# A four-layer graph kernel on one core: GpSimd clears an unused tile behind each indirect gather

## The chip, the cores and the metric

The kernel runs on one core of one Trainium2 chip. The metric is the device time of one execution in microseconds (us). The time shown for a kernel is the median of its timed runs; a separate execution is recorded by the hardware profiler, and all rows of the profile come from that one.

## The reference, cut to what matters

There are 16 graphs (b = 0 to 15) of 1024 nodes with 64 channels, and each has a sparse 1024x1024 adjacency. Four layers follow each other, each of the form x = layernorm(x + f(x, adj)).

```python
x = layernorm(x + (adj @ (x @ W) + bias))                       # layer 0
x = layernorm(x + L1(x, adj, nodemask))                         # layer 1, below
x = layernorm(x + proj(three times: h = relu(adj @ (h @ Wl + bl))))   # layer 2
x = layernorm(x + (adj @ x > 0.5))                              # layer 3
```

Layer 1 is the one that matters here. For each node it drops some neighbours by their rank (the "dilation"), sorts the remaining neighbours' values channel by channel, takes a weighted sum of three quantiles (0.25, 0.5, 0.75; a quantile between two sorted values is interpolated), adds the node itself, and applies a two-matrix perceptron with ReLU.

## The kernel before, in words

**Tiles.** The nodes of a graph are ranked by their number of neighbours and cut into eight tiles of 128 nodes. Tile t has room for KS[t] neighbours (31 down to 11). The tiles are worked in five groups per graph, `GROUPS = ((0,), (6, 7), (2, 3), (4, 5), (1,))`, so there are 80 groups in all.

**Steps of a graph.** `words_of` loads the adjacency, transposes it on TensorE, packs neighbours into words and does layer 0 (SP loads L417; TensorE L439, L464, L536; ScalarE L441, L539; VectorE L526). `front` makes the list of neighbours of each node (`idx`, `packed`) and writes the layer's input, with two extra columns that name the dropped neighbours, as a table to DRAM (L584). Then for each group:

- `gathered` (L808): GpSimd issues one indirect DMA per neighbour slot (L815). Each fetches 128 table rows of 66 floats, one for every node of the tile, into the group's buffer g. Slots that only few nodes use are fetched together into small `stage` tiles by the same helper; SP copies them to their places (L841) after VectorE has filled those places with a large number (L835).
- `masked` (L847): VectorE finds the dropped neighbours in the gathered rows (L862, L864), and ScalarE adds a large number to them (L868).
- `quantiles` (L891): VectorE runs a sorting network over the slots (L906), with s as its second buffer.
- `summed` (L916): ScalarE weighs the sorted slots (L932), TensorE adds them (L936), and the sum leaves PSUM (L949, L951).

`back` does the rest of layer 1 and layers 2 and 3 (TensorE L1207, L1141, L377; VectorE L1147).

**What sets the order.** Each step is a Python generator that yields the cost it expects; a heap with hand-set due times (`start`, `LENGTHS`, `add`) merges all generators into one program, so each engine has a fixed order of instructions, made before the run. A group's gathers are due two groups ahead of its sort. There are four g buffers for the 80 groups: the gathers of a group go into the buffer of the group four earlier and wait until its L936 (and L906) are done with it. GpSimd has nothing else to do in this stretch: its order is 2064 gathers in a row, 129 per graph (1952 into g, 112 into stage). Waits of a gather, where it has any: on the buffer, on the table, on the index list, and on the completion of the gather eight earlier, since the gathers use eight semaphores in turn.

Of the kernel before, what the change touches and what calls it, by code (L numbers as in the profile page):

```python
# [10 lines left out]
F32 = mybir.dt.float32  # L11
# [4 lines left out]
U8 = mybir.dt.uint8  # L16
# [4 lines left out]
P = 128  # L21
# [132 lines left out]
def kernel(  # L154
# [18 lines left out]
    nc = tc.nc  # L173
    B, N, C = x.shape
    H = w1.shape[1]
    NL = wl.shape[0]
    T = N // P
# [9 lines left out]
    const = ctx.enter_context(tc.tile_pool(name="const", bufs=1))  # L187
# [4 lines left out]
    act = ctx.enter_context(tc.tile_pool(name="act", bufs=1))  # L192
# [64 lines left out]
    top = const.tile([P, T, K], F32, name="top")  # L257
    nc.vector.memset(top, 0.0)
    flags = const.tile([1, B + 1], I32, name="flags")
    qw = const.tile([P, Q], F32, name="qw")  # L260
    ntau = const.tile([P, Q], F32, name="ntau")
    for s, (tau, w) in enumerate(zip(TAUS, QWEIGHTS)):
# [65 lines left out]

    mask_u8 = const.tile([B * T, P], U8, name="mask_u8")
    nc.scalar.dma_start(mask_u8, nodemask.rearrange("b (t p) -> (b t) p", p=P))  # L330
    mask_f = const.tile([B * T, P], F32, name="mask_f")
    nc.vector.tensor_copy(mask_f, mask_u8)
    mask = const.tile([P, B * T], F32, name="mask")
    pm = ps.tile([P, HALF], F32, tag="mm", name="pm", bufs=2)
# [447 lines left out]
    def group(g):  # L782

        n = max(KS[t] for t in GROUPS[g])
        lo, hi = RANKS[n]
        return GROUPS[g], n, lo, hi + 1 - lo

    def slots(g, buf, a, e):

        tiles, n, _, _ = group(g)  # L790
        return buf[:, :len(tiles) * n * R].rearrange("p (k t c) -> p t k c", k=n, c=R)[:, :, a:e, :]

    def packs_of(g):

        return [q for q, pack in enumerate(PACKS)
                if pack and g == min(h for h, tiles in enumerate(GROUPS) for p in pack if p[0] in tiles)]

    def shares_of(g):

        found = {}  # L800
        for q, pack in enumerate(PACKS):
            for t, k, m, first in pack:
                if t in GROUPS[g]:
                    found.setdefault((t, m, first, q // 2), []).append((q, k))
        return [(t, m, first, v[0][0], [k for _, k in v])
                for (t, m, first, _), v in sorted(found.items())]

    def gathered(st, g):  # L808
        tiles, n, _, _ = group(g)
        while "table" not in st:  # L810
            yield 0.5
        nt = len(tiles)
        st["g", g] = buf = srt.tile([P, KMAX * R], F32, tag="x", name="g", bufs=4)
        def gather(dst, index):
            nc.gpsimd.indirect_dma_start(  # L815
                out=dst, out_offset=None, in_=st["table"],
                in_offset=bass.IndirectOffsetOnAxis(ap=index, axis=0))

        whole = [(i, t, k) for i, t in enumerate(tiles) for k in range(n)
                 if k < len(ROWS[t]) and ROWS[t][k] == P]  # L820
        for j, (i, t, k) in enumerate(whole):
            if j == FIRST:
                for q in packs_of(g):
                    if q % 2 == 0:
                        st["stage", q // 2] = small.tile([P, 2 if PACKS[q + 1] else 1, R], F32,
                                                         tag=f"stage{q // 2}", name="stage", bufs=1)
                    gather(st["stage", q // 2][:, q % 2], st["packed"][:, q:q + 1])
                    yield 1.0
            gather(buf[:, (k * nt + i) * R:(k * nt + i + 1) * R], st["idx"][:, t, k:k + 1])
            yield 1.0  # L830
            if j == FIRST + LAG:
                for i2, t2 in enumerate(tiles):
                    full = ROWS[t2].count(P)
                    if full < n:
                        nc.vector.memset(slots(g, buf, full, n)[:, i2], BIG)  # L835
                for t2, m, first, q, ks in shares_of(g):

                    dst = buf[:m, :n * nt * R].rearrange("p (k t c) -> p k t c", t=nt, c=R)
                    dst = dst[:, ks[0]:ks[-1] + 1:max(ks[-1] - ks[0], 1), tiles.index(t2)]
                    src = st["stage", q // 2][first:first + m, q % 2:q % 2 + len(ks)]  # L840
                    nc.sync.dma_start(dst, src)  # L841

            st["in", g] = sum(j >= max(FIRST + LAG, max(x for x, w in enumerate(whole) if w[0] == i2))
                              for i2 in range(nt))
        st["all in", g] = True
# [403 lines left out]
    for b in range(B):  # L1249
        ready = start(b * G - 2) - BEFORE  # L1250
        add(ready - LISTS - WORDS, words_of(state[b]), WORDS / WORDS_STEPS)
        add(ready - LISTS - (LEAD if b else EARLY), front(state[b]), LISTS / LISTS_STEPS)
        add(start((b + 1) * G) + AFTER, back(state[b]), BACK / BACK_STEPS)
        for g in range(G):
            q = b * G + g
            st = state[b]
            count = sum(KS[t] for t in GROUPS[g])
            many = sum(ROWS[t].count(P) for t in GROUPS[g]) + len(packs_of(g))
            add(start(q - 2), gathered(st, g), (start(q - 1) - start(q - 2)) / (many + 1))
            half = (start(q) - start(q - 1)) * (PAIRS if len(GROUPS[g]) > 1 else MASKS)  # L1260
            add(start(q) - half, masked(st, g), 0.9 * half / (1.5 + 0.4 * count + 2.1 * len(GROUPS[g])))
            n = max(KS[t] for t in GROUPS[g])
            cost = 0.2 + sum((len(GROUPS[g]) * x[4] * x[8] * C + 151) / 960 for x in network(n))
            add(start(q), quantiles(st, g), (start(q + 1) - start(q)) / (cost + 0.1))
            add(start(q + 1) + SUMS, summed(st, g))
# [50 lines left out]
```

## Time and profile before

| What | Value |
|---|---|
| Timed runs | 3179.41 us median of 3 (3177.02 to 3182.76) |
| Span of the profiled execution | 4328.2 us |
| Mean granted TensorE clock in it | 0.764 |
| TensorE matmul busy | 2647.8 us, 61% |
| VectorE busy | 2822.0 us, 65% |
| ScalarE busy | 1914.0 us, 44% |
| GpSimd busy | 2160.8 us, 50% |

The profiled execution's own time is known only as its span, from its first to its last instruction; no time of it from outside is given. That span is 4328.2 - 3179.41 = 1148.8 us longer than the median of the timed runs, so shares of the span cannot be taken over to the timed runs as they are; durations of single instructions and the spacing of instructions on one engine are what is read from it. In rows of groups, "<-" in front of tiles means "written from", the number after x is the count, then come busy us, mean ns of one, and the idle time of the engine before them with what ended it. In timeline rows the columns are start us, us, engine, line, operation, tiles, count, and in brackets the idle time before. "issue" is idle time in which nothing that the profile shows was waited for; "remote" and "another core or an unknown queue" are waits whose releaser the profile could not name.

### The profile page before, as it was taken

To read this page: it belongs to the slowest core of one execution; us is meant where nothing else is said; L and a number is where in the kernel's file an instruction comes from. 1 tells how busy PE (TensorE), PEld (TensorE's weight loads), DVE (VectorE), ACT (ScalarE), POOL (GpSimd) and SP (SyncE) were. 2 spreads that over 40 slices of the span, in tenths; PEclk is the share of its full clock that TensorE was granted. 3 is DMA by queue.
4 is the path that set the end of the run, shared out by engine and by line. 5 is a ranking of instruction groups with operands and counts; after the bars stand their busy time and mean duration, and the time that the engine had idled before them with its cause. 6 is when DMAs were issued, how large, how long until landed. Compare 5 with 4: busy or idle time off the path is not lost.

```text
span 4328.2 us, 46055 instructions
## 1 busy us (share of the span) xinstructions
PE 2647.8 (61%) x13765; PEld 1635.7 (38%) x13766; DVE 2822.0 (65%) x6935; ACT 1914.0 (44%) x6153; POOL 2160.8 (50%) x2078
## 2 busy tenths in 40 slices
PE   6034285675848567584755758476575848456478
PEld 5023152443525244352533435253343525233243
DVE  6058383865849486594857668485766859476671
ACT  2034352634536264453535455363545536253641
POOL 1715626455454645546465464546545554645600
PEclk8566597787969778796877879687787969768688
DMA  3212121322222132222213222231322222111210
GB/s 107 42 50 70 34 67 37 104 54 78 73 71 84 40 101 56 78 77 74 77 39 90 64 83 76 65 84 40 100 60 79 78 80 71 39 57 24 62 43 3
DMA packets 169056, 282.54 MB, mean 65 GB/s; under 512 B 99485, under 2 KB 102112, under 8 KB 166880
## 3 DMA queue, kind: packets, MB, share of 16 engines
q1 hardware_dynamic: 67584, 142.01, 9.9%
q0 software_dynamic: 66048, 69.88, 9.1%
q10 hardware_dynamic: 35168, 67.62, 4.1%
q8 instruction: 114, 1.87, 0.2%
q14 instruction: 142, 1.16, 0.1%
HBM read 204.33 MB, written 71.44 MB: 64 GB/s over the span
## 4 chain that ended last, share of the span: by engine, by line
another core or an unknown queue 28%; DVE 25%; PE 23%; ACT 16%; issue 7%; DMA 0%; ACTq 0%; DVEq 0%
DVE g L906 7%; PE mm L1207 7%; DVE s L906 7%; ACT g L868 6%; ACT ones_at L974 3%; PE ax L464 3%; ACT ones_at L975 2%; PE tp L439 2%; PE mm L377 2%; PE pa L936 2%; PE mm L1196 2%; ACT g L932 1%; PE mm L1141 1%; DVE top L707 1%
## 5 line engine op out<-in xcount | busy, mean ns | idle before, releaser
L815 POOL DMA_INDIRECT g<-table,idx x1952 | 2045.4, 1048 | 1919.7 <-PE pa L936 666.8
L1207 PE MATMUL mm<-adjB,msg 128*128 128x512 f32 x1536 | 769.6, 621 | 109.1 <-issue 82.4
L936 PE MATMUL pa<-g,ident 128*128 128x128 f32 (+1 forms) x1600 | 376.0, 360 | 430.1 <-ACT g L932 300.5
L868 ACT ACTIVATE g<-g,bias 128x64 f32<-128x64 f32 (+9 forms) x2272 | 596.8, 341 | 47.9 <-DVE bias L864 29.2
L906 DVE TENSOR_TENSOR s<-g 128x256 f32<-128x256 f32 (+9 forms) x944 | 531.3, 588 | 64.5 <-ACT g L868 55.5
L936 PEld LDWEIGHTS pa<-g,ident 128*128 128x128 f32 x1600 | 312.3, 248 | 574.0 <-ACT g L932 347.1
L906 DVE TENSOR_TENSOR g<-s 128x256 f32<-128x256 f32 (+8 forms) x864 | 473.4, 573 | 9.0 <-DVE s L906 3.0
L932 ACT ACTIVATE g<-g,w 128x64 f32<-128x64 f32 x1552 | 397.8, 341 | 17.2 <-DVE w L912 13.6
L1207 PEld LDWEIGHTS mm<-adjB,msg 128*128 128x128 f32 x1536 | 268.7, 197 | 301.1 <-issue 270.7
L1147 DVE TENSOR_TENSOR u<-mm,mb 128x512 f32<-128x512 f32 x32 | 22.1, 691 | 463.1 <-remote 313.5
L464 PE MATMUL ax<-at,xt 128*64 128x128 f32 x1920 | 284.5, 310 | 17.4 <-issue 17.4
L377 PE MATMUL mm<-adjB,x 128*64 128x512 f32 x512 | 272.6, 666 | 36.3 <-issue 31.3
L979 PE MATMUL mm<-ones_at,pieces 128*64 128x512 bf16 x768 | 213.0, 420 | 119.0 <-ACT ones_at L975 77.1
L464 PEld LDWEIGHTS ax<-at,xt 128*64 128x64 f32 x1920 | 250.2, 158 | 81.2 <-issue 79.1
L439 PE MATMUL tp<-ident,arow 128*128 128x128 f32 x1024 | 181.7, 309 | 156.2 <-remote 66.4
L399 DVE TENSOR_REDUCE ln_v<-sq 128x8 f32<-128x512 f32 x64 | 43.6, 681 | 296.4 <-issue 156.8
L439 PEld LDWEIGHTS tp<-ident,arow 128*128 128x128 f32 x1024 | 140.9, 162 | 205.1 <-issue 131.7
L441 ACT COPY at<-tp 128x512 f32<-128x512 f32 x240 | 139.0, 580 | 177.2 <-remote 122.3
L906 DVE TENSOR_TENSOR g<-g,s 128x256 f32<-128x256 f32 (+5 forms) x432 | 199.1, 464 | 15.1 <-remote 5.0
L906 DVE TENSOR_TENSOR g<-g 128x256 f32<-128x256 f32 (+8 forms) x304 | 200.7, 660 | 11.2 <-remote 4.0
L1219 PE MATMUL mm<-ident,tT 64*128 64x64 f32 x128 | 25.7, 295 | 293.9 <-ACT tT L380 207.4
L1210 ACT ACTIVATE hlT<-mm 128x512 f32<-128x512 f32 x96 | 57.4, 598 | 296.4 <-PE mm L1207 123.7
(225 smaller groups left out, 4361.9 us busy)
## 6 DMA issues: line engine op xcount, KB each, us to landing
arow<-in_adj_dram SPq DMA_DIRECT2D x128, 512.0 KB
adjd<-at ACTq DMA_DIRECT2D x120, 512.0 KB
adjB<-adjd SPq DMA_DIRECT2D x15, 4096.0 KB
g<-table,idx POOLq DMA_INDIRECT x1952
table<-xc ACTq DMA_DIRECT2D x16, 264.0 KB
xt<-in_x_dram SPq DMA_DIRECT2D x16, 256.0 KB
out_dram<-y SPq DMA_DIRECT2D x16, 256.0 KB
stage<-table,packed POOLq DMA_INDIRECT x112
```

What stands on the lines that cost most here:

```text
L377: nc.tensor.matmul(pa[:C, :], src[:, m, :], adjT[:, h * TH:(h + 1) * TH, m, :], start=(m == 0), stop=(m == T - 1))
L439: nc.tensor.transpose(pt[:, i * P:(i + 1) * P], a[:, j * P:(j + 1) * P], ident)
L441: nc.scalar.copy(at[:, h * TH:(h + 1) * TH, :], pt.rearrange("p (i n) -> p i n", n=P))
L464: nc.tensor.matmul(self.bank[:C, cols], self.xt[:, m + 1, :], at[:, m, :], start=(m == 0), stop=(m == T - 1))
L815: nc.gpsimd.indirect_dma_start(out=dst, out_offset=None, in_=st["table"], in_offset=bass.IndirectOffsetOnAxis(ap=index, axis=0))
L868: nc.scalar.activation(v, v, AF.Identity, bias=bias[:m, i, k:k + 1])
L906: nc.vector.tensor_tensor(box(bufs[mode >> 1 & 1], d, run, sd, count), box(bufs[mode >> 3], a, run, sa, count), box(bufs[mode >> 2 & 1], b ...
L932: nc.scalar.activation(slots(g, bufs[0], lo + r, lo + r + 1)[:, i, 0, :C], slots(g, bufs[at[r]], lo + r, lo + r + 1)[:, i, 0, :C], AF.Iden ...
L936: nc.tensor.matmul(pa[:, :(e - k) * nt * C], ident, rows_.rearrange("p (k c) -> p k c", c=R)[:, :, :C], start=(j == 0), stop=(j == len(run ...
L974: nc.scalar.activation(ones_at, iota, AF.Abs, bias=st["minus"][:, s:s + 1])
L979: nc.tensor.matmul(bank[:C, :], pieces[:, i, s, :], ones_at[:, h * HALF:(h + 1) * HALF], start=(s == 0 and i == 0), stop=False)
L1207: nc.tensor.matmul(pg, msg[:, m, :], adjT[:, h * TH:(h + 1) * TH, m, :], start=(m == 0), stop=(m == T - 1))
```

## The change

The helper `gather`, which issues all indirect gathers, also issues a GpSimd memset of a tile named `pause`: 128 partitions of 256 bytes, type uint8, which nothing reads. There are as many memsets as gathers, 2064. To make room, a tile of constants that is used once at the start, `mask_f` (512 bytes per partition), moves from the pool of constants to a slot that is shared with the tiles tagged "u" of `back`.

```diff
@@ -257,6 +257,7 @@
     flags = const.tile([1, B + 1], I32, name="flags")
+    pause = const.tile([P, 2 * P], U8, name="pause")
     qw = const.tile([P, Q], F32, name="qw")
@@ -328,7 +329,7 @@
-    mask_f = const.tile([B * T, P], F32, name="mask_f")
+    mask_f = act.tile([B * T, P], F32, tag="u", name="mask_f")
     nc.vector.tensor_copy(mask_f, mask_u8)
@@ -815,6 +816,7 @@
             nc.gpsimd.indirect_dma_start(
                 out=dst, out_offset=None, in_=st["table"],
                 in_offset=bass.IndirectOffsetOnAxis(ap=index, axis=0))
+            nc.gpsimd.memset(pause, 0)
```

In the built program every gather is followed by one memset on GpSimd. Each memset but the first waits for GpSimd's own semaphore, since it overwrites what the memset before it wrote. The order of instructions on TensorE, VectorE, ScalarE and SP is the same as before.

## The prediction

> **What bounds the kernel now.** I read the page first, for busy shares and the chain of waits that ended last, then the groups of GpSimd, then its timeline, then a table of stretches.
>
> ```profile
> span 4328.2 us, 46055 instructions
> another core or an unknown queue 28%; DVE 25%; PE 23%; ACT 16%; issue 7%; DMA 0%; ACTq 0%; DVEq 0%
> ```
>
> On this page no engine bounds anything: the busiest is at 65%, and the longest part of the chain is waits without a named releaser. GpSimd, the only engine that the change touches, is not in the chain. But the profiled span is 1148.8 us longer than the timed median of 3179.41, and 28% of it, 1212 us, are those nameless waits. One of them in ScalarE's timeline:
>
> ```profile
> 107.53 0.33 ACTq L532 DMA_DIRECT2D adjd<-at  x1
> 165.70 0.21 ACT L539 CAST hi<-tp 128x64 f16<-128x64 f32 x1 [57.65 <-remote]
> ```
>
> L539 waits for matmuls (L536) that the records end at 108.2, and goes on at 165.7. GpSimd issues gathers all the while (110 in a row from 96.0 to 234.0). Such waits lie nearly all in runs of gathers. In the timed run they must be nearly absent, since 4328 - 1212 = 3116 is already below its 3179. So the engines' own pace, not the chain, says what bounds the timed run:
>
> ```profile
> L815 POOL DMA_INDIRECT g<-table,idx x1952 | 2045.4, 1048 | 1919.7 <-PE pa L936 666.8 <-issue 566.6 <-DVE s L906 272.9
> L815 POOL DMA_INDIRECT stage<-table,packed x112 | 113.0, 1009 | 35.0 <-issue 34.7 <-ACT at L441 0.3
> ```
>
> There are 2064 gathers, 2158 us of busy time and 601 us of "issue", about 0.3 us ahead of nearly every gather. The rest of the idle time, 1353 us, waits mostly for a free buffer (L936, L906). The stretches (busy us of PE, PEld, DVE, ACT, POOL with counts, then granted clock, DMA share, GB/s):
>
> ```profile
> 2156.40:2193.50 37.10, 34.67 (x184) 21.50 (x182) 35.81 (x74) 21.23 (x80) 29.43 (x26) 1.00 0.27 68
> 2197.00:2221.00 24.00, 5.42 (x23) 4.69 (x23) 0.00 (x0) 3.56 (x15) 18.19 (x20) 0.57 0.19 32
> 96.00:4116.00 4020.00, 2417.51 (x12660) 1498.03 (x12658) 2672.62 (x6485) 1821.06 (x5889) 2158.24 (x2064) 0.76 0.24 67
> 4116.00:4328.20 212.20, 171.41 (x557) 87.00 (x557) 83.54 (x208) 69.70 (x205) 0.12 (x1) 0.85 0.06 23
> ```
>
> Beside a busy VectorE (35.81 of 37.10 us) a gather is issued every 37.10/26 = 1.43 us; beside an idle one every 1.25 us (2217.54, 2218.79, 2220.03 in the timeline). The gathers begin at 96.0 and the last ends 212 us before the end. The timed run has the same edges if I take them over: 3179.4 - 96.0 - 212.1 = 2871 us are left for 2064 gathers, **1.39 us each**. That is less than the 1.43 of a dense stretch, and only 111 us more than what the profile's mean pace needs (2158 + 601 = 2760 us). So in the timed run GpSimd has nearly no slack. VectorE has little more: 2673 busy us of the 2871, 93%. Both are bounds; TensorE (2418) and ScalarE (1821) are behind.
>
> **The change, part by part.** (1) It removes nothing. (2) It adds 2064 memsets of 128x256 bytes to GpSimd, one between any two gathers. (3) It moves no instruction of another engine, since their order is fixed and is the same in both programs. (4) mask_f moves to a slot of the tag "u": VectorE's copy (L332) runs once at the start, and the slot's next user (L1147) first runs at 560 us. I cost this at nothing: the slot is empty in the first 500 us, which is its cover; without it, one copy would wait once.
>
> What one memset costs has no row. The nearest ones are GpSimd's first instructions:
>
> ```profile
> 0.34 0.10 POOL L1302 MEMSET const-float32-0.0<- 128x1 f32 x1
> 0.37 0.10 POOL L1302 MEMSET const-float32-1.0<- 128x1 f32 x1
> ...
> 1.08 0.97 POOL L212 IOTA iota<- 128x1024 f16 x1
> 2.03 0.28 POOL masks.py:199 TENSOR_SCALAR_AFFINE_SELECT ident<-ident 128x128 f32<-128x128 f32 x1
> 2.27 0.20 POOL L215 MEMSET tri<- 128x128 f16 x1
> 2.43 0.18 POOL L231 IOTA wordkey<- 128x64 int32 x1
> ```
>
> From one start to the next: 0.03 us for 1 element, 2.43 - 2.27 = 0.16 for 128, 0.95 for 1024. That is about 0.9 to 1.0 ns per element, and the 128x128 memsets last 0.205 us in f32 and 0.195 in f16, so elements count, not bytes. 256 elements then take 0.03 + 255 x 0.9 to 1.0 ns = 0.26 to 0.29 us; were it bytes, 256 of them are the 0.16 us of the f16 tile. I take 0.26. Bounds: nothing, if the memset falls into the 0.30 us of "issue" that is there anyway; and 0.26 + 0.30 = 0.56 us, if the memset gets such a gap of its own. The value nearest to the rows stands between; the ends are kept as rivals. Its wait is for the memset before, over a microsecond old, so it holds nothing up. Queued behind each memset is the next gather; who waits for that is the masking (L862, then L868), the SP copies from stage (L841), and so the sort (L906).
>
> The Trainium skill (Perfetto Trace Analysis, GPSIMD Engine Instruction) says that recorded spans of GpSimd are not to be trusted and that spacing of starts should be used; the tri memset shows it, 0.20 us long and 0.16 us to the next start. By durations the memset would be 0.10 + 255 x 0.75 ns = 0.29 us, and the sum 62 us higher. The skill (SBUF — State Buffer, Who interferes with whom) also says that a VectorE instruction with two SBUF inputs, which L906 is, holds up a GpSimd instruction that reads SBUF but not one that only writes; no row shows a memset beside a busy VectorE. If the rule failed and each memset were stretched as gathers are (1.43 - 1.25 = 0.18 us), it would cost 372 us more.
>
> **The sum.** 2064 x 0.26 = 537 us on GpSimd. What hides them: if gathers keep the profile's mean pace, 111 us of waits for buffers in the timed run, so 3179 + 537 - 111 = 3605. If GpSimd is already full, nothing but a small return: VectorE's 2673 us then lie in about 3340 us, 80% instead of 93%, and gathers get faster by 0.18/0.97 x 0.13 = 0.024 us, so 3179 + 2064 x (0.26 - 0.024) = 3666. I take the middle, **3635 us**. By the bytes' price of 0.16 it would be 3400 to 3460, by 0.29 3670 to 3730. GpSimd becomes the only bound; VectorE then idles at the masking step, waiting for gathers. In the profiled execution the same 537 us meet 1353 us of buffer waits, so its span may grow far less, and the sum is not to be read from it.
>
> **Rivals.**
>
> - *The memset hides in the gap.* If the 0.30 us ahead of a gather are the queue's work on it and run beside the memset, the pace grows by 0 to 0.1 us: 3179 to 3385. For it: the gap is constant (0.30 in nearly all rows). Against it: memsets and iotas at the start follow each other with no gap, so GpSimd's queue runs ahead of them and is not what they wait for.
> - *The change doesn't do what it says.* If timed gathers are faster than recorded ones, GpSimd has slack, VectorE is the bound, and the pauses only shorten buffer waits. It needs a pace below 1.39 - 0.26 = 1.13 us; the shortest in the trace is 1.25. Result: 3179.
> - *A gap of its own.* 0.56 us each: 3179 + 2064 x 0.56 - 111 = 4224; in part, 3850 and up.
> - *Faster.* The nameless waits lie in runs of gathers. If the timed run has some, spacing the gathers shortens them. Place: ScalarE's and VectorE's waits for TensorE. Price: VectorE's idle time between the first and last gather, 2871 - 2673 = 198 us at most; half of it gives 3080. It decides only if pace and pause together fit into 3080 - 308 = 2772 us, 1.34 us per gather, which needs a timed gather pace of 1.08 us with my memset, or 1.25 with a memset of 0.09. Against it: dense stretches run at 1.43.
>
> **Chances.** Paused and bound by GpSimd at 0.16 to 0.33 us per memset (3400 to 3800): 0.73. A gap of its own (3800 to 4224): 0.08. Hidden in the gap, at a cost that shows (3190 to 3400): 0.08. No difference: 0.04 (the second rival, and the first at its end). Faster: 0.07. A difference below 0.2% (6 us) can't be told from none. So faster 0.07, same 0.04, slower 0.89. The range is 3270 to 3880: it leaves out the faster and equal cases (0.11), half of the hidden case and half of the high one.
>
> **What would show it.** In the changed profile: a group of 2064 GpSimd memsets of about 0.3 us; starts of gathers 1.5 us apart beside an idle VectorE instead of 1.25 (1.25 again: the first rival); GpSimd's buffer waits falling from 1353 us; VectorE waiting at L862 for gathers; "remote" waits fewer or shorter, if spacing acts on them. I am wrong if the pace of gathers stays, or if the time falls below 3270: then GpSimd had slack that the recorded pace hides.

## The result and the profile after

The changed kernel takes 3572.27 us (median of 4 runs, 3562.70 to 3573.18), the kernel before 3179.95 us beside it (4 runs, 3177.02 to 3182.76): a ratio of 1.1225, 95% interval 1.1209 to 1.1241. The change makes it 392 us slower. The profiled execution of the changed kernel took 3562.7 us, with a span of 3560.9 us, so its shares can be taken over to the timed runs.

The kernel before took 3177 to 3180 us in four of the five sets of runs of this study and 4326 us in the fifth, and the profile shown of it above is of that upper level, so each experiment names the level that the kernel before had beside it.

The page of the changed kernel, its span, its chain, and the groups that the prediction spoke of (busy us, mean ns of one | idle us ahead of them, and what ended it):

```profile
span 3560.9 us, 48120 instructions
...
POOL 58%; DVE 21%; issue 8%; PE 8%; DMA 3%; ACT 1%; DVEq 0%; POOLq 0%; ACTq 0%; SPq 0%
...
L816 POOL DMA_INDIRECT g<-table,idx x1952 | 2140.8, 1097 | 414.3 <-issue 319.0
...
L819 POOL MEMSET pause<- 128x256 uint8 x2064 | 687.3, 333 | 1.2
...
L864 DVE TENSOR_SCALAR hits<-g,nself 128x38 f32<-128x38 f32 (+4 forms) x128 | 31.6, 247 | 453.3 <-DMA g<-table,idx 409.7
```

The longest waits of its gathers (us in total, times, longest):

```profile
POOL g L816 <- issue: 319.0, 1925, 0.3
POOL g L816 <- DVE nb L527: 90.3, 1, 90.3
POOL stage L816 <- issue: 18.7, 99, 1.9
POOL g L816 <- DVE s L908: 2.1, 13, 0.2
```

GpSimd now carries 58% of the chain, where it had none. The waits without a named releaser, 28% of the chain shown of before, are gone. Gathers hardly wait for a buffer any more: what is idle ahead of them is "issue" and some 90 us before the first one. In the profile of before, 1051 of the 1353 us were waits for a buffer (L936 and L906). This comparison is with a trace at the upper level, so it doesn't show what the change did: a trace without pauses at the lower level (third set) has neither kind of wait, and 6% of the chain on GpSimd. VectorE waits 409.7 us at the masking step for gathered rows. The pauses are recorded as 2064 x 0.333 us = 687 us, which is more than the 392 us that the change costs. GpSimd's timeline of the changed kernel shows why:

```profile
109.42 0.95 POOL L816 DMA_INDIRECT g<-table,idx  x1 [0.17 <-issue]
110.36 0.34 POOL L819 MEMSET pause<- 128x256 uint8 x1
110.86 0.95 POOL L816 DMA_INDIRECT g<-table,idx  x1 [0.17 <-issue]
111.81 0.33 POOL L819 MEMSET pause<- 128x256 uint8 x1
112.30 0.95 POOL L816 DMA_INDIRECT g<-table,idx  x1 [0.17 <-issue]
```

The memset starts as soon as the gather ends, but the gap of 0.30 us ahead of the next gather has shrunk to 0.17. From a gather's start to the next it is 1.44 us, against 1.25 without the memset: 0.19 us more and not 0.33. And 2064 x 0.19 is 392.

### The profile page after: what moved, and what is told of

Read it like the earlier page. It is cut to its first block, busy times and chain, and to the rows that moved or that the text cites. A ratio compares the mean times of both kernels' runs of the same rounds, so it can differ in the third digit from the quotient of the medians.

```text
span 3560.9 us, 48120 instructions
## 1 busy us (share of the span) xinstructions
PE 2549.5 (72%) x13765; PEld 1582.5 (44%) x13766; DVE 2838.6 (80%) x6935; ACT 1905.2 (54%) x6153; POOL 2954.4 (83%) x4142
## 4 chain that ended last, share of the span: by engine, by line
POOL 58%; DVE 21%; issue 8%; PE 8%; DMA 3%; ACT 1%; DVEq 0%; POOLq 0%; ACTq 0%; SPq 0%
POOL g L816 41%; POOL pause L819 13%; DVE g L908 7%; DVE s L908 7%; POOL stage L816 3%; PE mm L1209 2%; DMA g<-table,idx 2%; PE mm L378 1%; PE ax L465 1%; DVE top L708 1%; DVE nb L527 1%; DVE kw L711 1%; DMA adjB<-adjd 1%; PE pa L938 1%; PE mm L1198 0%
## 5 line engine op out<-in xcount | busy, mean ns | idle before, releaser
L816 POOL DMA_INDIRECT g<-table,idx x1952 | 2140.8, 1097 | 414.3 <-issue 319.0
L1209 PE MATMUL mm<-adjB,msg 128*128 128x512 f32 x1536 | 792.8, 637 | 21.5 <-ACT msg L1201 21.5
L819 POOL MEMSET pause<- 128x256 uint8 x2064 | 687.3, 333 | 1.2
L938 PE MATMUL pa<-g,ident 128*128 128x128 f32 (+1 forms) x1600 | 357.4, 353 | 302.9 <-ACT g L934 301.8
L908 DVE TENSOR_TENSOR s<-g 128x256 f32<-128x256 f32 (+9 forms) x944 | 530.4, 587 | 5.0
L908 DVE TENSOR_TENSOR g<-s 128x256 f32<-128x256 f32 (+8 forms) x864 | 473.5, 573 | 4.0
L864 DVE TENSOR_SCALAR hits<-g,nself 128x38 f32<-128x38 f32 (+4 forms) x128 | 31.6, 247 | 453.3 <-DMA g<-table,idx 409.7
L465 PE MATMUL ax<-at,xt 128*64 128x128 f32 x1920 | 267.7, 299 | 0.0
L378 PE MATMUL mm<-adjB,x 128*64 128x512 f32 x512 | 251.5, 625 | 5.5 <-DVE x L412 5.4
L908 DVE TENSOR_TENSOR g<-g 128x256 f32<-128x256 f32 (+8 forms) x304 | 200.2, 658 | 7.3
L908 DVE TENSOR_TENSOR g<-g,s 128x256 f32<-128x256 f32 (+5 forms) x432 | 198.4, 462 | 6.8
L537 PE MATMUL tp<-pow,nb 128*128 128x65 f16 x1024 | 60.7, 202 | 192.5 <-DVE nb L527 187.0
L981 PEld LDWEIGHTS <-pieces 128*64 128x64 bf16 x768 | 89.5, 118 | 193.8 <-issue 133.5
L888 ACT ACTIVATE hat<-iota,npos 128x10 f32<-128x10 f16 (+2 forms) x384 | 114.0, 297 | 110.5 <-DVE npos L877 110.4
```

What stands on the lines that cost most here:

```text
L378: nc.tensor.matmul(pa[:C, :], src[:, m, :], adjT[:, h * TH:(h + 1) * TH, m, :], start=(m == 0), stop=(m == T - 1))
L465: nc.tensor.matmul(self.bank[:C, cols], self.xt[:, m + 1, :], at[:, m, :], start=(m == 0), stop=(m == T - 1))
L816: nc.gpsimd.indirect_dma_start(out=dst, out_offset=None, in_=st["table"], in_offset=bass.IndirectOffsetOnAxis(ap=index, axis=0))
L819: nc.gpsimd.memset(pause, 0)
L888: nc.scalar.activation(h, iota[:, lo:lo + kw], AF.Abs, bias=npos[:, i, s:s + 1])
L908: nc.vector.tensor_tensor(box(bufs[mode >> 1 & 1], d, run, sd, count), box(bufs[mode >> 3], a, run, sa, count), box(bufs[mode >> 2 & 1], b ...
```

## The experiments

There were two theories at the start. **Pace**: in the timed run GpSimd issues gathers without a rest, so every gather costs what the pause adds between two gathers, and nothing else matters. **VectorE**: it is the real bound at 93%, and the pauses lengthen the run by what they do to it, or to the signals that it waits for. The expectations state them in their own terms, for each kernel. The diffs are against the changed kernel, and "..." stands for lines left out.

### First set: the kernel before at 4326 us

Beside these four the kernel before took 4326.24 us (19 runs, 4298 to 4349), the upper level.

**The moved tile alone** (the change without its memsets):

```diff
                 in_offset=bass.IndirectOffsetOnAxis(ap=index, axis=0))
-            nc.gpsimd.memset(pause, 0)
```

> The change without its memsets: only the unused tile and the moved mask_f stay. Theory A (GpSimd's pace is the bound, and all of the added time is the memsets): 3180 us, as before. Rival (the moved tile or the shifted addresses have a part in it): anything off 3180 by over 10 us. For the profile: if the nameless waits of the profiled execution of before belong to gathers that follow each other without a pause, its span is again several hundred us over its timed runs; if they belonged to that one execution, the span is within 10 us of the time.

Measured: 4332.4 us, ratio 1.0002 (0.9966 to 1.0037). The move of mask_f costs nothing. The level itself was the surprise. The page of this kernel, and its list of waits (us in total, times, longest):

```profile
span 4338.3 us, 46055 instructions
...
another core or an unknown queue 28%; PE 25%; DVE 23%; ACT 16%; issue 7%; DMA 0%; ACTq 0%; DVEq 0%
```

```profile
POOL g L816 <- PE pa L937: 671.0, 44, 82.7
POOL g L816 <- issue: 567.6, 1861, 0.6
...
ACT hi L540 <- remote: 289.0, 23, 59.6
```

This is the picture of the kernel before as it was shown: nameless waits of up to 60 us, most of them on ScalarE and VectorE, some in lines such as L540 that read what TensorE wrote, and GpSimd waiting for buffers. Added up over the trace they come to 1736 us (174 waits). 99% of that is in waits that begin, and 87% of it passes, while gathers follow each other in a run with gaps below 2 us; such runs fill 69% of the time from the first gather to the last.

**One element instead of 256:**

```diff
-            nc.gpsimd.memset(pause, 0)
+            nc.gpsimd.memset(pause[:, :1], 0)
```

> The memset clears one element per partition in place of 256. Theory A: the time is 93 + 170 us of edges plus 2064 times the pace of a gather with its pause. With a gather of 1.10 us, the gap of 0.165 us that the changed profile shows ahead of a gather, and a memset of 0.10 us, the pace is 1.365 us, against 1.405 before, so 3080 us, down to where VectorE binds (about 3100), and no slower than 3200. Rival B (before, GpSimd had some 100 us of slack and VectorE set the time): 3180, no gain from a shorter pace. Rival C (an instruction between two gathers costs by being there, through its wait): 3400 and more.

Measured: 4389.5 us, ratio 1.0145 (1.0068 to 1.0222).

**The same bytes in fewer elements:**

```diff
+U32 = mybir.dt.uint32
...
-    pause = const.tile([P, 2 * P], U8, name="pause")
+    pause = const.tile([P, P // 2], U32, name="pause")
```

> The memset clears the same 256 bytes per partition as 64 uint32 elements. If elements set its length: 0.33 us falls to 0.10 + 64 x 0.9 ns = 0.16 us, the pace is 1.10 + 0.165 + 0.16 = 1.425 us, and the time 3205 us. If bytes set it: 0.33 us and 3572 us as in the changed kernel.

Measured: 4287.4 us (median of ten runs, 4235.6 to 4318.9). The ratio, 0.9863 (0.9820 to 0.9906), goes by the six shortest of them.

**Twice the elements:**

```diff
-    pause = const.tile([P, 2 * P], U8, name="pause")
+    pause = const.tile([P, 4 * P], U8, name="pause")
```

> The memset clears 512 elements in place of 256. Theory A: 256 elements more at 0.9 ns are 0.23 us, the pace rises from 1.60 to 1.83 us, and the time from 3572 to 4040 us, with no waits on GpSimd. Rival B (slack was used up first, so the first 256 elements were partly free): 0.26 us or more per memset, 4110 us and up.

Measured: 3991.4 us, ratio 0.9230 (0.9181 to 0.9278): faster than the kernel before, which stood at its upper level. GpSimd's timelines, first one element:

```profile
110.80 0.94 POOL L816 DMA_INDIRECT g<-table,idx  x1 [0.19 <-issue]
111.74 0.12 POOL L819 MEMSET pause<- 128x1 uint8 x1
112.05 0.94 POOL L816 DMA_INDIRECT g<-table,idx  x1 [0.19 <-issue]
```

then 64 elements of 4 bytes:

```profile
110.93 0.95 POOL L817 DMA_INDIRECT g<-table,idx  x1 [0.16 <-issue]
111.89 0.17 POOL L820 MEMSET pause<- 128x64 uint32 x1
112.21 0.95 POOL L817 DMA_INDIRECT g<-table,idx  x1 [0.16 <-issue]
```

and 512 elements:

```profile
109.35 0.95 POOL L816 DMA_INDIRECT g<-table,idx  x1 [0.17 <-issue]
110.30 0.54 POOL L819 MEMSET pause<- 128x512 uint8 x1
111.01 0.95 POOL L816 DMA_INDIRECT g<-table,idx  x1 [0.17 <-issue]
```

With the pause of one element the starts stay 1.25 us apart, although it is recorded as 0.12 us: a pause doesn't cost by being there (rival C), nor does it shorten the pace, as theory A had it. The table takes the median distance from a gather's end to the next one's start, over all 2064:

| Pause | Recorded length (median) | End of gather to next start | Added |
|---|---|---|---|
| none | | 0.305 us | |
| 1 element | 0.120 us | 0.305 us | 0 |
| 64 elements of 4 bytes | 0.166 us | 0.329 us | 0.024 us |
| 256 elements of 1 byte (the change) | 0.325 us | 0.491 us | 0.186 us |
| 512 elements of 1 byte | 0.539 us | 0.705 us | 0.400 us |

So elements count and not bytes: 64 elements of 4 bytes hold the same 256 bytes as the change's pause and add 0.024 us instead of 0.186. The slope is (0.705 - 0.491) / 256 = 0.84 ns per element, and the same from 64 to 256. Some 0.14 us of each longer pause (0.325 - 0.186; 0.539 - 0.400) run inside a gap that is there anyway.

The traces also part in the nameless waits. They come to 1591 us with one element and 1522 us with 64, but to none at all with 512, where the starts are 1.66 us apart. In the times of the first three kernels those waits and the pauses are mixed, so no price of a pause can be read from them. The kernel with 512 elements has no such wait, so its time is its pace alone; it is taken up below.

### Second set: fewer pauses, the kernel before at 3177 us

The same chip number, 18 minutes later: the kernel before took 3176.8 us (7 runs, 3176.0 to 3182.6).

**The changed kernel again.**

> The changed kernel once more, unaltered, beside the kernel before on the chip of this call. Theory A, GpSimd's pace: 93 + 170 + 2064 x 1.60 = 3565 us on any chip, since no nameless wait is in its profile. What the kernel before does on this chip is the question: if its time is near 4330 again, the ratio is 0.825, and the nameless waits are part of its timed runs too; if it is near 3180, the ratio is 1.12.

Measured: 3563.8 us, ratio 1.1211 (1.1193 to 1.1230).

**A pause behind every second, fourth and eighth gather** (shown for 2; 4 and 8 in the others):

```diff
+    pauses = [0]
...
-            nc.gpsimd.memset(pause, 0)
+            pauses[0] += 1
+            if pauses[0] % 2 == 0:
+                nc.gpsimd.memset(pause, 0)
```

> The memset follows every second gather. Theory A with openings that need not follow each gather: 1032 pauses of 0.195 us, 201 us, are added to the 3180 of a run without nameless waits: 3380 us, wherever before stands at 4330 or 3180. Rival (each gather needs its own opening, or the nameless waits come back): over 3900 us where before stands at 4330.

> The memset follows every fourth gather. If openings this far apart (5.2 us) are enough: 516 pauses of 0.195 us, 3280 us. If the nameless waits come back where before has them: between 3600 and 4330 us.

> The memset follows every eighth gather. If an opening each 10 us is enough: 258 pauses, 3230 us. The late completions in the first run of gathers of before came 11 us apart, so I expect the nameless waits back here: about 4200 us where before stands at 4330; 3230 us where it stands at 3180.

| Kernel | Pauses | Time | Ratio (95% interval) | Over 3176.8 | First to last gather | Gathers' own durations, summed |
|---|---|---|---|---|---|---|
| every eighth | 258 | 3202.8 us | 1.0075 (1.0059 to 1.0092) | 26 | 2939.2 us | 2260.7 us |
| every fourth | 516 | 3230.7 us | 1.0168 (1.0151 to 1.0185) | 54 | 2962.1 us | 2234.1 us |
| every second | 1032 | 3345.6 us | 1.0527 (1.0510 to 1.0545) | 169 | 3078.5 us | 2250.2 us |
| every one | 2064 | 3563.8 us | 1.1211 (1.1193 to 1.1230) | 387 | 3296.7 us | 2268.9 us |

Even the fewest pauses cost time, though all three thinned kernels came out below the theory's figures. By 0.186 us each their pauses are 48, 96 and 192 us, and all of them 384. Only all of them together are paid in full; with fewer, the gathers' own durations fall by 12 to 38 us against the 2272.4 us that they sum to without any pause (third set, below). The space between gathers grows by 46, 95 and 196 us for the first three, about as the price says; what is missing is in the gathers themselves, and why they get shorter is open. GpSimd waits for no buffer in any of them worth telling.

### Third set: VectorE, the kernel before at 3177 us

**The moved tile alone, once more.**

> The kernel without its memsets once more (the same as e1_no_memset), to have its profile where the kernel before takes about 3180 us, if this call's chip does that. Expected there: 3178 us, no nameless waits, gathers of 1.10 us with gaps of 0.305 us in one unbroken row, 2064 x 1.405 = 2900 us plus 97 + 170 us of edges = 3167 us, so GpSimd's waits for buffers below 50 us in all. Rival (GpSimd had slack, VectorE set the time): buffer waits of 100 us and more, and VectorE busy over 97% between the first and the last gather. Where before stands at 4330, again 4330 with nameless waits.

Measured: 3175.4 us, ratio 0.9995 (0.9985 to 1.0004), beside 3177.2 us of the kernel before. Program and instruction count are those of the first experiment, which took 4332 us. So this trace is what was missing: the kernel before, but for one tile's place, at its lower level. Page, then waits of VectorE, then waits of GpSimd:

```profile
span 3172.4 us, 46055 instructions
...
PE 41%; DVE 34%; ACT 13%; POOL 6%; issue 4%; DMA 1%; DVEq 0%; ACTq 0%; POOLq 0%
```

```profile
DVE u L1148 <- PE mm L1142: 78.3, 4, 60.6
DVE hits L863 <- DMA g<-table,idx: 46.8, 8, 17.5
```

```profile
POOL g L816 <- issue: 567.3, 1861, 0.5
POOL g L816 <- DVE nb L528: 94.3, 2, 94.0
POOL stage L816 <- issue: 31.4, 103, 0.3
POOL g L816 <- DMA g<-table,idx: 14.5, 37, 1.6
```

No nameless wait is left, and no buffer wait: apart from the 94 us before the first gather, GpSimd is either issuing or in the 0.305 us that follow every gather. Yet the chain gives it only 6%: it goes back mostly through TensorE and VectorE. The masking step waits 46.8 us for gathers, which is 409.7 in the changed kernel. The stretch from the first gather's start to the last one's end (busy us of PE, PEld, DVE, ACT, POOL with counts, then granted clock, DMA share, GB/s), first here, then in the changed kernel:

```profile
97.13:3002.28 2905.15, 2305.76 (x12788) 1434.57 (x12786) 2704.59 (x6551) 1831.93 (x5982) 2272.40 (x2064) 0.88 0.34 92
```

```profile
93.41:3391.14 3297.73, 2365.27 (x12814) 1470.06 (x12813) 2719.68 (x6552) 1838.93 (x5987) 2951.66 (x4128) 0.83 0.28 81
```

Without pauses GpSimd needs 2272.4 + 2063 x 0.305 = 2901.6 of the 2905.2 us: it has some 4 us of slack. VectorE is busy for 93% of that stretch, and for 82% with the pauses; TensorE's matmuls for 79% and 72%.

The two rows also bear on two other ways in which the pauses could have cost time. VectorE's own instructions take 15 us more with the pauses (2719.7 against 2704.6), so it isn't that the memsets held VectorE up. The granted TensorE clock is lower (0.83 against 0.88) and the matmuls take 60 us more, but GpSimd waits for TensorE nowhere in that stretch by more than a fraction of a microsecond, so the longer row of gathers doesn't come from there.

**Work added to VectorE, none to GpSimd**, and **work added to both:**

```diff
-            nc.gpsimd.memset(pause, 0)
+            nc.vector.memset(pause[:, :64], 0)
```

```diff
+    late = const.tile([P, P // 2], U8, name="late")
...
             nc.gpsimd.memset(pause, 0)
+            nc.vector.memset(late[:, :64], 0)
```

> In place of GpSimd's memset, VectorE clears 64 bytes of the unused tile at each gather's place in the schedule, 2064 times about 0.11 us, 230 us of VectorE work that nothing waits for (the nearest row of VectorE is a memset of 132 f32 elements, 0.168 us). Theory A (before, GpSimd is the bound and VectorE at 93% is next): some 200 us fit into VectorE's idle time, so 3180 to 3300 us where before is 3180. Rival B (VectorE set the time before): 3180 + 230 = 3410 us.

> The changed kernel with the same 2064 small VectorE memsets as well. Theory A (with the pauses GpSimd alone is the bound, VectorE idles some 570 us between first and last gather): 3572 us, at most 30 us more. Rival (the added time came from VectorE being held up by GpSimd's memsets, so that VectorE is still the bound): 3572 + 230 = 3800 us.

Measured: 3183.3 us, ratio 1.0022 (1.0012 to 1.0031), for VectorE alone, and 3538.2 us, ratio 1.1137 (1.1119 to 1.1156), for both. Groups of VectorE and GpSimd of the first, and of GpSimd of the second:

```profile
L819 DVE MEMSET pause<- 128x16 uint32 x2064 | 148.6, 72 | 2.3
```

```profile
L816 POOL DMA_INDIRECT g<-table,idx x1952 | 2139.8, 1096 | 711.4 <-issue 568.1 <-DVE nb L528 93.3 <-DVE g L908 23.1
```

```profile
L817 POOL DMA_INDIRECT g<-table,idx x1952 | 2101.9, 1077 | 416.7 <-issue 318.7 <-DVE nb L529 93.0 <-DVE s L910 2.3
L820 POOL MEMSET pause<- 128x256 uint8 x2064 | 700.0, 339 | 1.2
```

As many extra instructions on VectorE cost 6 to 8 us, and on GpSimd 387 to 392. VectorE's are recorded as 148.6 us, but much of each lies beside its neighbour: all of VectorE's busy time grows by 2862.9 - 2824.3 = 38.6 us. So the test is weaker than its count of instructions suggests; still, 38.6 us more on VectorE gave 6 to 8, where 258 pauses worth 48 us on GpSimd gave 26. It also brought back a first wait for a buffer, 23.1 us at L908. With VectorE's memsets on top of the pauses the kernel was not slower but some 26 us faster than the changed kernel, because gathers became shorter (1077 ns instead of 1097; 41 us in all). VectorE was busy 45 us longer there than in the changed kernel (2883.5 against 2838.6), so a kernel bound by VectorE should have been slower. That gathers became shorter wasn't foreseen, and why is open.

### Fourth set: the changed kernel a third time

> The changed kernel once more, beside the kernel before. Theory (GpSimd's pace sets the time, and at 1.44 us from start to start no TensorE signal is late): 3564 +- 10 us, whichever of its two levels (3177 or 4326 us) the kernel before shows here, so a ratio of 1.12 at the one and 0.82 at the other. Rival (the pause only lengthens the pace, and the late signals come with the place where the kernel runs): the same 3564 us where the kernel before takes 3177, but well over 4326 us where the kernel before takes 4326.

Measured: 3564.7 us beside 3176.5 us, ratio 1.1224 (1.1205 to 1.1243). The kernel before stood at its lower level, so the two theories weren't told apart: the changed kernel was never run beside the upper level.

## Why the prediction was right, point by point

**What bounds the kernel: right.** "GpSimd has nearly no slack" is what the third set shows, with 4 us of slack in 2905. "In the timed run they must be nearly absent" held for the nameless waits: none in the trace at 3172 us. It was argued from 4328 - 1212 = 3116, which only shows that all of the chain's nameless waits can't be in a run of 3179 us, and it is a statement on the lower level only. That such waits "lie nearly all in runs of gathers" is right for where they begin; as such runs fill 69% of the stretch, it says less of the cause than it seems.

**The hidden slack of 111 us: wrong, and it is a mis-sized term.** The prediction took the mean pace of the profile at 4328 us, (2158 + 601) / 2064 = 1.34 us. At that level VectorE often stood still, so many gathers ran at their short 0.95 us. At 3172 us, 1885 of the 2064 gathers have VectorE busy for over nine tenths of their time (1174 at 4328 us); all 2064 last 1.101 us on average and the pace is 1.408: 2905 us for 2064, with some 4 us of slack in place of 111. The second of its two sums, "GpSimd is already full", was the right one, and the middle between them was not needed. The tail was 170 us and not 212, which with the longer gather stretch cancels out.

**The price of a memset, 0.26 us: wrong in size.** Measured: 0.186. The trace records 0.333 us, and the distance between gathers says 0.186, because 0.14 us of it pass in the old gap. The first rival, "the memset hides in the gap", was thus half true, and it was turned down with a poor reason: that the instructions at the start of the program follow each other without a gap says nothing of the gap behind a gather. The rival "a gap of its own" was the opposite of what happened. The price by elements was right (0.84 ns against the 0.9 to 1.0 assumed), and so was that bytes don't count. The Trainium skill (Perfetto Trace Analysis, GPSIMD Engine Instruction) advises to go by the spacing of starts and not by spans, and here the difference is large: by spans 2064 x 0.333 = 687 us, by starts 2064 x 0.19 = 392.

**The return of 0.024 us per gather: absent.** VectorE's share fell from 93% to 82%, as forecast, but the sum of the gathers' durations went from 2272.4 to 2269.7 us only. With fewer pauses it did fall, by up to 38 us. What sets a gather's stretch beside VectorE isn't its busy share alone; the runs don't show what it is. The memset itself is hardly stretched: its median is 0.325 us and its mean 0.333, 16 us in all, while the gathers' go from 0.95 to 1.10. In the trace of the changed kernel, 785 pauses ran beside VectorE's sorting instructions (L908) alone and 324 beside an idle VectorE: both average 0.328 us, and none of them is longer than 0.337. The 248 that met a TENSOR_SCALAR average 0.369 and reach 0.772, which is 11 of the 16 us. Of the gathers, 412 ran beside L908 alone and average 1.123 us, the 317 beside an idle VectorE 0.951. For the memset beside the sort, this agrees with what the Trainium skill says (SBUF — State Buffer, Who interferes with whom): a VectorE instruction with two SBUF inputs gets in the way of a GpSimd instruction that reads SBUF, not of one that only writes it.

**The sum.** Against the trace at 3172.4 us: gathers' durations -2.7, the space between gathers 1028.0 - 632.7 = +395.3 (2063 x 0.186 = 383, the rest mostly stretched pauses), the first gather 3.7 earlier, the tail 0.3 shorter. That makes up the 388.5 us by which the spans differ (3560.9 - 3172.4), and nearly all of it lies between gathers. Against the 3572 us of its own set, the forecast of 3635 was 63 us too high: the price of 0.26 put in 2064 x 0.074 = 153 us too much, and the slack and the return, taken at the middle of 111 and 49, took out some 80 us that didn't exist. That these errors partly cancelled is luck; the mechanism, GpSimd without rest paying for each pause, isn't.

**The move of mask_f at nothing: right**, in both sets (1.0002 and 0.9995).

**The rival "faster": wrong where it was asked, but not empty.** Its mechanism, nameless waits that spacing shortens, may exist at the upper level: the other three traces of that set have 1522 to 1736 us of nameless waits, the one with the 512-element pause has none, at a cost of 2064 x 0.40 = 826 us, and that kernel ends 7.7% below the kernel before. From the kernel at its lower level the same price gives 3177 + 826 = 4003, against 3991 measured, so its time is what its pace alone gives. That the spacing took the waits away is the likely reading, from one spacing in one set. If the changed kernel, which took 3564 to 3572 us in its three sets, kept that time beside the upper level, it would be some 18% faster there. That wasn't measured.

**Is there a better version?** None of these kernels beats 3177 us: each number of pauses that was timed beside the lower level cost time, and the shorter pauses, of one element and of 64, were timed only beside the upper level.

## What to carry to other kernels

Price an instruction put between two gathers by the distance from start to start, with a short and a long one of it, since the first 0.14 us were free here and the rest cost 0.84 ns per element. An engine that never rests in its stretch (4 us of slack in 2905) pays for additions even where the chain of waits gives it 6%, here in full with all pauses and about half with the fewest (26 of 48 us): look at the engine's own idle time before the share. And where a profiled execution is a third longer than the timed ones, find a trace at the timed level before taking mean paces from it, since they carried the 111 us of slack that didn't exist.

## What the runs showed of the hardware that was not expected

**Two levels of the same program.** The kernel without pauses ran at 4332 us in one set and at 3175 in another, each time with all its runs together and equal to the kernel before. At the upper level ScalarE's cast of TensorE's results (L540) waits without a named releaser for 289.0 us (23 times, up to 59.6); at the lower one the same line waits for TensorE by name:

```profile
L540 ACT CAST hi<-tp x128: 186/207/222, 15.8 to 2683.5; 128x64 f16<-128x64 f32 x128
  PE tp L537: 68.1, 45
```

That is 68.1 us in all (45 times). At the upper level 99% of the nameless waits, by time, begin inside runs of gathers, which are 1.25 us apart from start to start beside an idle VectorE. They are also there at 1.25 and 1.28 us with the shortest pauses; at 1.66 us there are none. This would fit signals of TensorE that arrive late while GpSimd issues gathers closely, in some sets of runs only; as the traces name no releaser, it is not shown. Whether it is the place where the program runs, what else is at work there, or something that the recording adds, no run here tells; both levels were seen on a chip of the same number.

**A gather's cost.** Issuing one gather of 128 rows takes 0.95 us beside an idle VectorE and 1.11 to 1.14 on average beside a busy one (over nine tenths of its time), and 0.305 us pass before the next gather can start. A short instruction on GpSimd can use 0.14 us of that gap.
